# Projecting from a transposed input: five of eight blocks of a fused attention and mixture-of-LoRA layer

## The chip, the core and the metric

The kernel runs on one core of a Trainium2 chip. A core has a matrix engine (TensorE, "PE" in the profile; its weight loads are "PEld"), a vector engine (VectorE, "DVE"), a scalar engine (ScalarE, "ACT"), a general engine (GpSimd, "POOL") and a queue engine (SyncE, "SP") that here issues all DMAs. Each engine works through its own instructions in order; semaphores tie them together. The metric is the device time in microseconds of one execution, as the median of several runs. The profile is that of one execution.

## The reference

The input x has 2 sequences of 2048 rows of 512 numbers. All is in 32-bit floats. The layer is

```python
x = x + attention(layernorm(x), Wq, Wk, Wv, Wo)     # 16 heads of 32, causal, rotary positions
x = x + ffn(layernorm(x), base_w, base_b, router_w, router_b, lora_A, lora_B)
```

`layernorm` takes the mean from each row and divides by sqrt(variance + 1e-5). In the attention, q, k and v are the normalised rows times the transposed weights; q and k are then turned by position:

```python
rot = jnp.stack([t1 * cos - t2 * sin, t1 * sin + t2 * cos], axis=-1)
```

The feed-forward part is one dense product plus, for each row, the two best of eight LoRA experts, chosen by a softmax router.

## The kernel before

The 4096 rows are worked in eight blocks of 512 (four tiles of 128): blocks 0 to 3 are the first sequence, 4 to 7 the second. Block n has `j = n % 4`, and its queries look at the `j + 1` key blocks of their own sequence. The 16 heads are worked four at a time (index `g`, 0 to 3, one group of 32 rows of the matrix array for each head), so there are 32 head steps (n, g).

For each block, `prepare` (line 211) makes the normalised input with the channels on the partitions. `load` brings a tile of x; `measured` calls `moments` (line 175), which takes mean and variance on DVE, raises variance + eps to the power -0.5 on POOL and makes the shift -mean x factor on POOL; `scaled` normalises on ACT (line 189); `turned` makes four 128x128 transposes on TensorE (line 208) and copies the result from PSUM to `xnt_a` on ACT (line 209). `project` then makes keys and queries of one head group: 16 products of 128x32 weights in four column groups (line 201; after a turn in the same phase they run as four full products, line 196). The result is turned by position with a shuffle and a product with cosine on DVE (lines 251, 252) and a product with sine and a sum on POOL (lines 253, 254). `value` projects a tile of values and copies it from PSUM in four pieces on ACT (line 271).

For each head step, `row_maxima` makes all scores once to find the row maxima (line 424 on TensorE, line 442 on DVE), and `attend` makes them again the other way round (line 585), takes exponentials on ACT (line 627) into one of three `pt` buffers, multiplies them with the values (line 665) and adds them up on POOL (line 715); their sums go through DRAM (`sums`, `few`, `over`, lines 737 to 748) and come back to scale the result (line 750). `finish` (line 280) does the output projection, the second layer norm, the router and the feed-forward product of a block that has all its heads. Scores, projections and all other products take turns in seven PSUM banks, handed out in rotation; the weighted values have an eighth.

The order of the instructions on TensorE, ACT and DVE is the order in which the program writes them. A planner writes it: the work of the scores is cut into phases (`phase`, `begin[k]` the first phase of head step k), and everything else is put between them. `set_aside(at, do)` does something at a given phase; `wait([(us, do)], at, not_before)` gives work for TensorE with an estimated time, a due phase and an earliest phase, taken when there is credit for it or when it is due. The queues of POOL and SP are ordered by the compiler.

`start_block` (line 856) sets a block's preparation: with `at` the block's first phase and `lead` at most 12, but less where the last head step of the block before is short, tiles are loaded from phase `at - lead - 14`, measured two phases later, scaled two more later and turned from `at - lead - 9`; the projections can begin at `at - lead - 6`. `xnt_a`, `cos` and `sin` have one buffer each, so a block's load of them waits for the last use in the block before. The tag `tmp`, with six buffers, holds tiles of x, the shuffled projections, normalised rows of the feed-forward part and the sums. The tag `w`, one buffer of 1 MB, holds `wo` and `base_w` in turn.

Of the kernel before, what the change touches and what calls it, by code (L numbers as in the profile page):

```python
# [12 lines left out]
ALU = mybir.AluOpType  # L13
# [21 lines left out]
def preln_attention_moe_lora(  # L35
    ctx: ExitStack,
    tc: tile.TileContext,
    x: bass.AP,
    wq_t: bass.AP,
    wk_t: bass.AP,  # L40
# [128 lines left out]
    def load_in_turn(src, name):  # L169
# [3 lines left out]
        return w  # L173

    def moments(xt, t, name):

# [33 lines left out]

    def prepare(n):

        j = blocks[n][1]
        made = {"q": [], "k": [], "v": []}
        held = {"x": [], "by": []}

        def load(t):
            held["x"].append(first_x[t] if n == 0 else load_x(n, t, False))  # L220
            if t == NT - 1:
                held["turn"] = first_turn if n == 0 else load_turn(j)

        def measured(t):
            held["by"].append(moments(held["x"][t], t, f"a{n}"))

# [29 lines left out]
        def value(t):  # L256
# [13 lines left out]
            for g in range(NC):  # L270
                nc.scalar.copy(made["v"][g][:, t, :], pv[:, bass.ts(g, P)])

# [4 lines left out]
        ]  # L277
        return (load, measured, scaled, turned), heads, [[(3.6, lambda t=t: value(t))] for t in range(NT)], made

# [576 lines left out]
    def start_block(n):  # L856

        (load, measured, scaled, turned), heads, vals, made = prepare(n)
        keys[n], values[n], queries[n], contexts[n] = made["k"], made["v"], made["q"], []
        at, j = begin[NC * n], blocks[n][1]  # L860

        lead = min(LEAD, at - begin[NC * n - 1] - 6) if n > 0 else 0
        for t in range(NT):
            if n > 0:
                set_aside(at - lead - EARLY + t, lambda t=t: load(t))
                set_aside(at - lead - EARLY + 2 + t, lambda t=t: measured(t))
                set_aside(at - lead - EARLY + 4 + t, lambda t=t: scaled(t))
                wait([(0.5, lambda t=t: turned(t))], at - lead - 8 + t, at - lead - 9 + t)
            else:
                load(t)  # L870
        if n == 0:
            for do in (measured, scaled, turned):
                for t in range(NT):
                    do(t)
            make_masks_of_maxima()
        for g in range(NC):
# [10 lines left out]
            if g == 1:  # L887
                for stage in vals:
                    wait(stage, begin[NC * n + 1] + 1, at - lead - 6)

    def end_block(n):
# [7 lines left out]

    EARLY, BEHIND, LEAD = 14, 3, 12  # L900
    start_block(0)
# [123 lines left out]
```

## Time and profile before

| | us |
|---|---|
| median of three runs | 1772.98 (1772.81 to 1774.18) |
| the profiled execution | 1771.69 |
| its span, first to last instruction | 1769.6 |
| TensorE busy | 1735.1 |
| DVE busy | 1016.9 |
| ACT busy | 763.5 |
| POOL busy | 1368.4 |
| granted TensorE clock | 0.997 of full |

The first row is the metric. The profile stands for one execution, whose own time is in the second row. Busy shares are means over the whole span: an engine with 77% can be the one that ends last in a stage, and an engine with 98% can have stages in which it waits.

In lines of groups, "x128 | 22.5, 305 | 8.4 <-ACT" reads: 128 instructions, 22.5 us busy together, 305 ns each, 8.4 us of idle time of the engine just before them, most of it ended by what follows the arrow. Matmuls overlap in the array, so their lengths add up to more than the time they take.

### The profile page before, as it was taken

The numbers are of one execution on the slowest core, as the hardware profiler recorded it, in microseconds if no ns is written. First come the engines' busy times: TensorE is split into PE (matmuls) and PEld (weight loads), VectorE is DVE, ScalarE is ACT, GpSimd is POOL, SyncE is SP. The second block draws the span as 40 slices with busy tenths as digits, with TensorE's granted clock in tenths as the row PEclk, the third lists the DMA queues.
The fourth block names the chain that finished last, engine by engine and source line by source line (L and its number), as shares of the span: only waits on it lengthen the run. The fifth ranks groups of instructions, "written<-read, shape, count | busy, mean of one in ns | idle before, by whom it ended". The sixth has DMA issues, their size and how long they took to land.

```text
span 1769.6 us, 45671 instructions
## 1 busy us (share of the span) xinstructions
PE 1735.1 (98%) x19482; PEld 694.9 (39%) x19482; DVE 1016.9 (57%) x2359; ACT 763.5 (43%) x1600; POOL 1368.4 (77%) x878
## 2 busy tenths in 40 slices
PE   8999999999999999999999999999999999999998
PEld 3444444333433334433343434333343433434333
DVE  4555655566657656564555556466565576666504
ACT  1434443345434535354542424334344445455371
POOL 3647766699797899899974478567996798999951
PEclk9999999999999999999999999999999999999999
DMA  5000101002110002200010121110022000010101
GB/s 191 20 15 21 61 26 56 8 8 67 45 36 8 8 2 67 71 10 2 20 33 14 44 73 62 43 44 4 14 71 67 1 9 8 2 32 20 61 8 48
DMA packets 42307, 61.91 MB, mean 35 GB/s; under 512 B 13180, under 2 KB 13692, under 8 KB 42104
## 3 DMA queue, kind: packets, MB, share of 16 engines
q1 hardware_dynamic: 42104, 59.00, 10.7%
q8 instruction: 152, 2.49, 0.6%
q14 instruction: 51, 0.42, 0.1%
HBM read 50.08 MB, written 8.90 MB: 33 GB/s over the span
## 4 chain that ended last, share of the span: by engine, by line
PE 45%; DVE 2%; POOL 1%; issue 1%; ACT 1%; DVEq 0%; POOLq 0%
PE sm L424 9%; PE av L665 8%; PE yps L196 4%; PE sc L585 4%; PE sc L609 4%; PE ops L201 3%; PE qps L201 3%; PE kps L201 2%; PE vps L201 2%; PE den L705 1%; PE yps L201 1%; PE sc L595 1%; POOL pt L715 1%; DVE pm L442 1%; PE mid L196 1%
## 5 line engine op out<-in xcount | busy, mean ns | idle before, releaser
L715 POOL TENSOR_TENSOR pt<-pt,pt 128x1024 f32<-128x1024 f32 (+3 forms) x544 | 1078.5, 2007 | 202.5 <-ACT pt L627 193.6
L627 ACT ACTIVATE pt<-sc 128x512 f32<-128x512 f32 (+1 forms) x1152 | 595.2, 573 | 804.7 <-PE sc L585 651.8
L442 DVE TENSOR_REDUCE pm<-sm 128x1 f32<-128x512 f32 (+3 forms) x1280 | 710.7, 604 | 346.8 <-PE sm L424 183.7
L424 PE MATMUL sm<-k,q 32*128 32x512 f32 (+3 forms) x2560 | 653.5, 571 | 2.4 <-ACT xnt_a L209 1.2
L585 PE MATMUL sc<-q,k 32*128 32x512 f32 (+3 forms) x2560 | 557.1, 540 | 0.0
L665 PE MATMUL av<-pt,v 128*32 128x256 f32 (+3 forms) x3392 | 317.1, 452 | 2.1 <-ACT ctx L684 1.4
L424 PEld LDWEIGHTS sm<-k,q 32*128 32x128 f32 x2560 | 246.4, 183 | 51.9 <-issue 28.8
L609 PE MATMUL sc<-max,ones_b 3*128 3x512 bf16 (+3 forms) x1648 | 211.8, 306 | 3.4 <-DVE pm L442 2.8
L585 PEld LDWEIGHTS sc<-q,k 32*128 32x128 f32 x2560 | 207.0, 185 | 5.6 <-issue 4.4
L665 PEld LDWEIGHTS av<-pt,v 128*32 128x32 f32 x3392 | 70.0, 108 | 242.7 <-issue 190.1
L609 PEld LDWEIGHTS <-ones_b 3*128 3x128 bf16 x1648 | 61.3, 91 | 184.7 <-issue 182.7
L201 PE MATMUL qps<-xnt_a,wq 128*32 128x512 f32 x992 | 114.0, 600 | 0.9 <-ACT pt L627 0.9
L201 PE MATMUL ops<-wo,ctx 128*32 128x512 f32 x896 | 101.1, 594 | 0.0
L201 PE MATMUL vps<-wv,xnt_a 128*32 128x512 f32 x864 | 97.9, 594 | 0.0
L201 PE MATMUL kps<-xnt_a,wk 128*32 128x512 f32 x800 | 90.9, 594 | 0.0
L196 PE MATMUL yps<-base_w,xnt_f 128*128 128x512 f32 x200 | 90.3, 594 | 0.6 <-DVE pm L442 0.6
L595 PEld LDWEIGHTS <-which 32*128 32x128 bf16 x2048 | 38.8, 91 | 120.2 <-issue 95.3
L253 POOL TENSOR_TENSOR sw_q<-sw_q,sin 128x512 f32<-128x512 f32 x32 | 41.0, 1281 | 53.6 <-DVE sw_q L251 53.6
L433 PEld LDWEIGHTS <-which_q 32*128 32x128 bf16 x2048 | 65.1, 92 | 25.1 <-issue 17.1
L253 POOL TENSOR_TENSOR sw_k<-sw_k,sin 128x512 f32<-128x512 f32 x32 | 40.9, 1279 | 40.5 <-DVE sw_k L251 40.5
L433 PE MATMUL sm<-past_q,which_q 32*128 32x32 bf16 x2048 | 70.3, 173 | 0.0
L386 DVE TENSOR_TENSOR xf<-yps,xf 128x512 f32<-128x512 f32 x32 | 22.1, 692 | 82.4 <-PE yps L196 52.4
(110 smaller groups left out, 1324.4 us busy)
## 6 DMA issues: line engine op xcount, KB each, us to landing
xa<-in_x SPq DMA_DIRECT2D x32, 256.0 KB
xf<-in_x SPq DMA_DIRECT2D x32, 256.0 KB
wo<-in_wo_t SPq DMA_DIRECT2D x8, 1024.0 KB
base_w<-in_base_wt SPq DMA_DIRECT2D x8, 1024.0 KB
out<-xf SPq DMA_DIRECT2D x32, 256.0 KB
sum<-over SPq DMA_DIRECT2D x124, 64.0 KB
cos<-in_cos SPq DMA_DIRECT2D x8, 256.0 KB
sin<-in_sin SPq DMA_DIRECT2D x8, 256.0 KB
```

The costliest lines, as they stand in the source:

```text
L196: nc.tensor.matmul(out=out, lhsT=lhsT, rhs=rhs, start=start, stop=stop)
L201: nc.tensor.matmul(out=out[rows, :], lhsT=lhsT[:, rows], rhs=rhs, start=start, stop=stop)
L253: nc.gpsimd.tensor_mul(sw, sw, held["turn"][1])
L424: nc.tensor.matmul(out=sc[r][:, some[i]], lhsT=q[rows, bass.ts(ts[i], P)], rhs=keys[c][rows, : wide_of[i]], start=(i == 0), stop=(c != j),)
L433: nc.tensor.matmul(out=sc[r][:, at : at + DK], lhsT=which_q[rows, DK * (3 - m) : DK * (3 - m) + P], rhs=past_q[rows, :], start=False, stop ...
L442: nc.vector.reduce_max(pm[:, t, r, c : c + 1], sc[r][:, here], axis=AX.X)
L585: nc.tensor.matmul(out=sc[r][:, place(kts[i])], lhsT=keys[jj][rows, bass.ts(tt, P)], rhs=q[rows, low(kts[i]) :], start=first(r), stop=(r n ...
L595: nc.tensor.matmul(out=sc[r][:, at : at + DK], lhsT=which[rows, DK * (3 - c) : DK * (3 - c) + P], rhs=past[rows, :], start=first(r), stop= ...
L609: nc.tensor.matmul(out=sc[r][:, at:end], lhsT=ones_b[rows, :], rhs=s["max"][rows, here : here + end - at], start=first(r), stop=(r in held ...
L627: nc.scalar.activation(pt[:, r, all_of], sc[r][:, all_of], AF.Exp, scale=1.0 / math.sqrt(DK))
L665: nc.tensor.matmul(out=s["av"][rows, lo:hi], lhsT=values[jj][g][:, tt, rows], rhs=pts[kt][:, r, at + lo : at + hi], start=(kt == 0 and lo ...
L715: nc.gpsimd.tensor_add(some, some, pts[kt][:, r : r + 2, place(kt)])
```

## The change

Five blocks (those with `lead` above 0: 2, 3, 4, 6 and 7) no longer turn normalised rows. A second copy of x, transposed by the host, is given as `x_t`; its 512 columns of the block are loaded straight to `xnt_a` (1 MB). They are neither centred nor scaled. Layer norm's mean is taken out of the weights instead: Wq, Wk and Wv are centred over their input channels on the chip once, in place, during block 1. For each weight, POOL adds the four chunks, TensorE multiplies the sum with ones, and DVE subtracts the mean. The factor 1/sqrt(variance + eps) of each row is still found from tiles of x (which are loaded two phases earlier and no longer scaled). It is written to DRAM as a row, read back on all 128 partitions and multiplied into the block's cosine and sine on POOL, which scales keys and queries; the values are scaled in their copy from PSUM. Blocks 0, 1 and 5 keep the old way.

```diff
+    def centre(w, name):
+        some = wide.tile([P, NC, D], F32, tag="w", name=f"some_{name}")
+        nc.gpsimd.tensor_add(some[:, :2, :], w[:, :2, :], w[:, 2:, :])
+        nc.gpsimd.tensor_add(some[:, 0, :], some[:, 0, :], some[:, 1, :])
+        def centred():
+            mean = bank(f"mean_{name}")
+            product(
+                out=mean, lhsT=one.to_broadcast([P, P]), rhs=some[:, 0, :], start=True, stop=True
+            )
+            nc.vector.scalar_tensor_tensor(
+                w, mean.unsqueeze(1).to_broadcast([P, NC, D]), -1.0 / D, w, ALU.mult, ALU.add
+            )
+        return centred
...
+        def load_turned():
+            held["xn_t"] = wide.tile([P, NC, BLK], F32, tag="xnt_a", name=f"xnt_a{n}")
+            nc.sync.dma_start(
+                out=held["xn_t"],
+                in_=x_t[:, bass.ds(b * S + j * BLK, BLK)].rearrange("(c p) s -> p c s", p=P),
+            )
...
+            rstd = held["rstd"][:, t : t + 1]
+            nc.vector.bn_stats(both[:, :n6], held["x"][t])
+            nc.vector.bn_aggr(both[:, n6:], both[:, :n6])
+            nc.vector.tensor_scalar_add(rstd, both[:, n6 + 1 : n6 + 2], EPS)
+            nc.gpsimd.tensor_tensor(rstd, rstd, power, ALU.pow)
+
+        def spread():
+            row = dram.tile([P, NT], F32, name=f"row_{n}")
+            nc.sync.dma_start(out=row, in_=held["rstd"])
+            held["row"] = p2.tile([P, BLK], F32, tag="tmp", bufs=6, name=f"rows_{n}")
+            nc.sync.dma_start(
+                out=held["row"],
+                in_=row.rearrange("(o p) t -> o (p t)", o=1).to_broadcast([P, BLK]),
+            )
+
+        def weighted_turn():
+            by = held["row"].rearrange("q (p t) -> q t p", t=NT)
+            for turn_of in held["turn"]:
+                some = turn_of.rearrange("q (t p) -> q t p", t=NT)
+                nc.gpsimd.tensor_mul(some, some, by)
...
             for g in range(NC):
-                nc.scalar.copy(made["v"][g][:, t, :], pv[:, bass.ts(g, P)])
+                if flat:
+                    nc.scalar.activation(
+                        made["v"][g][:, t, :], pv[:, bass.ts(g, P)], AF.Copy,
+                        scale=held["rstd"][:, t : t + 1],
+                    )
+                else:
+                    nc.scalar.copy(made["v"][g][:, t, :], pv[:, bass.ts(g, P)])
...
+        lead = min(LEAD, at - begin[NC * n - 1] - 6) if n > 0 else 0
+        flat = lead > 0
...
+            if flat:
+                set_aside(at - lead - EARLY - 2 + t, lambda t=t: load(t))
+                set_aside(at - lead - EARLY + t, lambda t=t: measured(t))
+            elif n > 0:
...
+        if flat:
+            set_aside(at - lead - EARLY + 3, spread)
+            set_aside(at - lead - EARLY + 5, load_turned)
+            set_aside(at - lead - 6, weighted_turn)
...
+        if n == 0:
+            for i, w in enumerate((wk, wq, wv)):
+                held = []
+                first = CENTRED + 4 * i
+                set_aside(first, lambda w=w, i=i, held=held: held.append(centre(w, i)))
+                wait([(0.9, lambda held=held: held.pop()())], first + 4, first + 2)
...
-    EARLY, BEHIND, LEAD = 14, 3, 12
+    EARLY, BEHIND, LEAD, CENTRED = 14, 3, 12, 22
...
+        "x_t": given("attn_x").reshape(B * S, D).T,
```

More of the change, by code (lines that the diff above doesn't have):

```diff
@@ L38, in preln_attention_moe_lora @@
     x: bass.AP,
+    x_t: bass.AP,
     wq_t: bass.AP,
@@ L209, in turn, with prepare @@
         nc.scalar.copy(xn_t[:, :, bass.ts(t, P)], tp.rearrange("p (c q) -> p c q", c=NC))
-    def prepare(n):
-        j = blocks[n][1]
+    def prepare(n, flat):
+        b, j = blocks[n]
         made = {"q": [], "k": [], "v": []}
@@ L222, in load @@
                 held["turn"] = first_turn if n == 0 else load_turn(j)
-        def measured(t):
-            held["by"].append(moments(held["x"][t], t, f"a{n}"))
+        def load_turned():
[4 more added lines that the diff above has]
+            )
+        def measured(t):
+            if not flat:
+                held["by"].append(moments(held["x"][t], t, f"a{n}"))
+                return
+            if t == 0:
+                held["rstd"] = small.tile([P, NT], F32, tag="rstd", bufs=1, name=f"rstd_{n}")
+            n6, n2 = nc.vector.BN_STATS_DIM, nc.vector.BN_AGGR_DIM
+            both = small.tile([P, n6 + n2], F32, tag="mom", bufs=4, name=f"mom_a{n}_{t}")
+            rstd = held["rstd"][:, t : t + 1]
[16 more added lines that the diff above has]
+                nc.gpsimd.tensor_mul(some, some, by)
         def scaled(t):
@@ L277, in prepare @@
         ]
-        return (load, measured, scaled, turned), heads, [[(3.6, lambda t=t: value(t))] for t in range(NT)], made
+        return (load, load_turned, measured, spread, weighted_turn, scaled, turned), heads, [[(3.6, lambda t=t: value(t))] for t in range(NT)], made
     def finish(n, ctx_t):
@@ L856, in start_block @@
     def start_block(n):
-        (load, measured, scaled, turned), heads, vals, made = prepare(n)
-        keys[n], values[n], queries[n], contexts[n] = made["k"], made["v"], made["q"], []
         at, j = begin[NC * n], blocks[n][1]
         lead = min(LEAD, at - begin[NC * n - 1] - 6) if n > 0 else 0
+        flat = lead > 0
+        pieces, heads, vals, made = prepare(n, flat)
+        load, load_turned, measured, spread, weighted_turn, scaled, turned = pieces
+        keys[n], values[n], queries[n], contexts[n] = made["k"], made["v"], made["q"], []
         for t in range(NT):
-            if n > 0:
+            if flat:
+                set_aside(at - lead - EARLY - 2 + t, lambda t=t: load(t))
+                set_aside(at - lead - EARLY + t, lambda t=t: measured(t))
+            elif n > 0:
                 set_aside(at - lead - EARLY + t, lambda t=t: load(t))
```

## The prediction

> **What bounds the kernel now.** I read the page first: span and busy shares, then the slices, then who waits for whom, then the groups of one shape each, then the time lines of the places that the change touches.
>
> ```profile
> span 1769.6 us, 45671 instructions
> PE 1735.1 (98%) x19482; PEld 694.9 (39%) x19482; DVE 1016.9 (57%) x2359; ACT 763.5 (43%) x1600; POOL 1368.4 (77%) x878
> POOL 3647766699797899899974478567996798999951
> ```
>
> TensorE (PE) is busy for 98% of the span, so work taken from it is time taken, unless something else ends last in that stage. POOL has an average of 77%, but slices of 9 in which it could be that something else. Next the groups:
>
> ```profile
> L208 PE MATMUL xnps_a<-ident,xa 128*128 128x128 f32 x128 | 22.5, 305 | 8.4 <-ACT xa L189 7.8 <-DVE three L454 0.2
> L209 ACT COPY xnt_a<-xnps_a 128x512 f32<-128x512 f32 x32 | 18.6, 592 | 7.3 <-PE xnps_a L208 7.2
> L189 ACT ACTIVATE xa<-xa,mom_a 128x512 f32<-128x512 f32 x32 | 26.4, 825 | 6.1 <-POOL mom_a L185 5.7 <-DVE mom_a L183 0.2
> L271 ACT COPY v<-vps 128x128 f32<-128x128 f32 x128 | 24.8, 279 | 102.1 <-PE vps L201 88.6 <-PE vps L196 13.4
> L715 POOL TENSOR_TENSOR pt<-pt,pt 128x1024 f32<-128x1024 f32 x360 | 846.1, 2381 | 146.9 <-ACT pt L627 143.0 <-DVE pt L516 1.2 <-PE av L665 1.2
> L253 POOL TENSOR_TENSOR sw_k<-sw_k,sin 128x512 f32<-128x512 f32 x32 | 40.9, 1279 | 40.5 <-DVE sw_k L251 40.5
> L252 DVE TENSOR_TENSOR k<-kps,cos 128x512 f32<-128x512 f32 x32 | 21.6, 675 | 0.0
> L185 POOL TENSOR_SCALAR mom_a<-mom_a 128x1 f32<-128x1 f32 x32 | 8.6, 268 | 3.2
> L344 ACT ACTIVATE ex<-logits,neg 128x8 f32<-128x8 f32 x32 | 10.3, 321 | 0.0
> ```
>
> The first line is what the change mostly removes. TensorE's time line shows what one of these turns costs where it stands:
>
> ```profile
> 468.81 0.40 PE L665 MATMUL av<-pt,v 128*32 128x256 f32 x4
> 469.14 0.66 PE L208 MATMUL xnps_a<-ident,xa 128*128 128x128 f32 x4
> 469.73 0.39 PE L609 MATMUL sc<-max,ones_b 3*128 3x512 bf16 x2
> ```
>
> The columns are start, length, engine, line. The av product ends at 469.21 and the next product begins at 469.73: four transposes put 0.52 us between them, less than their own 0.66, because both ends overlap.
>
> **Which blocks.** `lead` is min(12, phases in the last head step of the block before, less 6). It is 0 for blocks 1 and 5 (the blocks before them have one tile row) and above 0 for 2, 3, 4, 6, 7. These five lose 20 of the 32 turns. In the trace their turns begin at 219, 467, 763, 1091 and 1339 us.
>
> **The sum, term by term** (minus is time gained).
>
> 1. Transposes in blocks 2, 3, 6, 7: 16 x 0.52 = -8.3 us. All lie on TensorE.
>
> 2. Transposes in block 4: 4 x 0.52 = 2.1 us of TensorE, but here POOL ends last:
>
> ```profile
> 755.00:830.00 75.00, 73.76 (x796) 26.34 (x792) 42.56 (x82) 38.43 (x82) 73.89 (x44) 1.00 0.02 5
> ```
>
> This row of busy times by stage has PE, PEld, DVE, ACT, POOL: POOL is busy for 73.89 of 75 us, and just after that TensorE stands idle (2.46 us at 839.7 among others), while ScalarE (ACT) waits 4.87 us for POOL at 848. The change gives POOL two products of 128x512 (L253: 2 x 1.28 = 2.56) and takes four shifts (L185: 4 x 0.27, and some 0.1 idle after each, 1.5 in all). So POOL is 1.1 us later and TensorE 2.1 earlier. POOL was idle for 2.28 us at 830-832, which gives back part. I take -0.8; ends -2.1 and +1.1. One operand of those products steps 16 bytes, which no row here shows; L253 (both operands contiguous, 1.28 us) is the nearest row.
>
> [...]
>
> 3. Waits that go with the turns: TensorE idle 1.16 us at 227.9 (scores behind `xnt_a`, ACT's copy L209), 0.15, 0.08 and 0.15 us before turns (for L189), and 1.7 us at 1093 behind an ACT queue in which a removed L189/L209 pair (0.83 + 0.59) stood ahead of the feed-forward's copy, of which I take half: 1.16 + 0.37 + 0.85 = -2.4. Ends: 0 (next in line is VectorE's (DVE) row maximum, named at 230.3) and -3.2.
>
> 4. Three products for the weights' means: each is one chunk in four column groups, like a `den` product, which the chain shows as "0.86 PE den L705 x8" at 1692.38. 3 x 0.86 = +2.6, all on TensorE.
>
> 5. Three subtractions on DVE over 2048 columns, one operand in PSUM. L252 takes 675 ns for 512; the reductions (L442: 279 ns for 128, 684 for 512) give 1.055 ns a column; 675 + 1536 x 1.055 = 2.3 us each. Queued behind each are the row maxima that free the score banks, and TensorE waits for those. By the planner's due times they fall at phases 24 to 34, at about 119, 130 and 148 us. In 119-127 DVE is busy 7.41 of 8 us, so there most of 2.3 shows; I take 1.5. At 130 a 3.6 us projection on TensorE follows and DVE is then idle 3.73 us; 0.5. At 148 a projection has just ended; 0.5. Sum +2.5; ends 0 and 6.9.
>
> 6. POOL's sums of weight chunks, 2.38 (L715, 1024 columns) + 1.27 (512) = 3.65 us, three times, one to two phases ahead of the mean that needs them. POOL is busy 30.1 of 54 us at 105-159, with 9.0 us idle before 125.44: 0. Without that cover TensorE stands up to 3.65 each.
>
> 7. The row of factors. Four `pow` on POOL remain. Then 2 KB go out through SP's queue, come back as 256 KB, then POOL's two products, then the first key projection's product with cosine on DVE (L252), which had no POOL ahead of it. The sums' way through DRAM is the same kind of trip: `over` issued at 167.33, the next issue released at 168.80, 1.5 us; a 256 KB load moves at some 250 GB/s (209-215 us), 1 us: about 4 us with issues. The code leaves five phases, 2.6 us each at 763-771: 13 us. Next is POOL's own queue. In block 4 `sw_k` was ready at 777.8 and POOL came to it at 783.14, a backlog of 5.3 us, and DVE wants cosine at 777.73. The products stand about two POOL additions (4.7 us) ahead of that place, so cosine would be done at about 779.7, 2 us late; maxima behind it have slack, 0.8 to 0.9 us between them. I take +0.5; ends 0 and 5.3. At 250 and 470-475 us POOL is idle, so blocks 2, 3 (and 6, 7, alike) pay 0.
>
> 8. The values' copies become ACTIVATEs with a scale from memory. L344, 8 columns with one operand of that kind, takes 321 ns; the copies of 128 and 512 columns (279, 592) extrapolate to 181, so 0.14 us more each, 0.56 for the four of one tile, 20 times: 11 us more on ACT, against 20 x (0.83 + 0.59) = 28 less. Off the path, but exponentials queue behind them: +0.5; ends -2 and +3.
>
> 9. Loads. Five of 1 MB through SP; `base_w`, of the same size, was issued at 209.10 and the traffic falls off by 215-217. The x loads go two phases earlier and keep their buffers only until the statistics. The 1 MB load waits for the previous block's last read of `xnt_a`, three phases before first use, with `sums`, `over` and `out` behind it on SP. 0; end +3 in block 4, where the first projection follows soonest.
>
> -8.3 - 0.8 - 2.4 + 2.6 + 2.5 + 0 + 0.5 + 0.5 + 0 = -5.4 us. The profiled execution took 1771.69 (1769.6 span and 2.1 around it), so 1766.3 by its own time. It stood 1.3 below the median of the three runs shown; against that median the forecast is 1772.98 - 5.4 = **1767.6 us**.
>
> **The rivals.**
>
> *The gain is eaten.* Row maxima late behind all three subtractions (term 5 at 6.9 in place of 2.5) give 1772.0. For it: DVE 93% busy at 119-127. Against it: seven banks and the idle 3.73 us. Within 0.2%.
>
> *Slower: POOL stands at the two products.* They wait on a DMA in an in-order queue; SP, in order too, may hold the row behind a load that waits for its buffer. It did so before: SP issued at 198.52 and then nothing until 206.56, for the sine tile. All additions behind stop, and with three `pt` buffers ACT and TensorE follow. Place: the first phases of each flat block's lead. Price: the lateness past 13 us of slack, times five; from (5.4 + 3.5) / 5 = 1.8 us each it decides. 4 us each give 1787.6 less what POOL's idle time absorbs, say 1780. Against it: POOL waits for DMA at L750 only 18.2 us in 14 times, 2.5 at most.
>
> *Larger gain.* Terms 5, 7 and 8 at their favourable ends (0, 0, -2) and term 3 at -3.2: 1772.98 - 11.7 = 1761.3. For it: ACT is 17 us lighter just where feed-forward and projection share its queue.
>
> *It does not do what it says:* the planner gives less early filler, TensorE waits for maxima where a transpose stood. Terms 1 and 2 halve: 1772.1, counted with the eaten gain.
>
> **How the numbers follow.** Forecast 0.52, larger gain 0.12, eaten 0.16, slower 0.20. 0.2% of the time (3.5 us) is about what a measurement of this kernel tells from no change; below 1769.4 counts as faster. So faster 0.64, same 0.16, slower 0.20. The likeliest case alone spans 1763 to 1771. Leaving out some 0.06 below and 0.14 above, the range is 1759 to 1778.
>
> **What would show it.** [...] Wrong would be: DVE or POOL named in TensorE's waits at the flat blocks' first keys, POOL idle for a DMA at the new products, or SP standing still for longer than before.

## The result and the profile after

| | us |
|---|---|
| before, median of six runs beside it | 1772.89 (1771.46 to 1774.35) |
| after, median of six runs | 1783.67 (1781.66 to 1788.91) |
| ratio, 95% interval | 1.0069 (1.0059 to 1.0079) |
| the profiled execution after | 1787.35, span 1785.5, granted clock 0.996 |

The change makes the kernel 0.6 to 0.8% slower, some 11 us, where 5.4 us less was forecast. The page of after, span and busy times:

```profile
span 1785.5 us, 45395 instructions
PE 1730.9 (97%) x19360; PEld 687.4 (38%) x19360; DVE 1022.9 (57%) x2362; ACT 746.8 (42%) x1560; POOL 1388.5 (78%) x874
```

ACT is busy 17 us less, as the forecast had it. TensorE is busy 4 us less, where 7.8 follow from terms 1, 2 and 4 (10.4 - 2.6); the span is 16 us longer. So the loss is idle time and clock, not work. The groups of after that answer to the forecast's:

```profile
L226 PE MATMUL xnps_a<-ident,xa 128*128 128x128 f32 x48 | 9.3, 334 | 18.6 <-ACT xa L207 18.4 <-DVE three L511 0.2
L227 ACT COPY xnt_a<-xnps_a 128x512 f32<-128x512 f32 x12 | 6.7, 585 | 4.1 <-PE xnps_a L226 4.0
L207 ACT ACTIVATE xa<-xa,mom_a 128x512 f32<-128x512 f32 x12 | 9.8, 815 | 2.2 <-POOL mom_a L203 1.9 <-DVE mom_a L201 0.2
L323 ACT ACTIVATE v<-vps,rstd 128x128 f32<-128x128 f32 x80 | 22.9, 368 | 52.1 <-PE vps L219 41.4 <-PE vps L214 10.7
L187 DVE SCALAR_TENSOR_TENSOR wq<-mean,wq 128x2048 f32<-128x2048 f32 x1 | 2.3, 2281 | 0.0
L276 POOL TENSOR_TENSOR cos<-cos,rows 128x512 f32<-128x512 f32 x5 | 7.7, 1543 | 15.5 <-DMA rows<-row 13.2 <-DMA sum<-over 2.3
L179 POOL TENSOR_TENSOR some<-wk 128x1024 f32<-128x1024 f32 x1 | 2.3, 2339 | 7.9 <-DMA wk<-in_wk_t 7.9
```

The first five lines are as forecast: 48, 12 and 12 instructions are left, the subtraction takes 2.3 us, a value copy 368 ns (279 ns and 0.14 us more were forecast). The last two are not. POOL stands 15.5 us in front of its five cosine products, and 7.9 us in front of the first sum of weight chunks. TensorE's first line shows 18.6 us of waiting where there were 8.4 (for ACT 18.4, where there were 7.8).

**The start.** The time line of after, POOL first, then DVE, then TensorE:

```profile
1.43 0.30 POOL masks.py:199 TENSOR_SCALAR_AFFINE_SELECT ident<-ident 128x128 f32<-128x128 f32 x1
9.60 2.34 POOL L179 TENSOR_TENSOR some<-wk 128x1024 f32<-128x1024 f32 x1 [7.87 <-DMA wk<-in_wk_t]
11.89 1.03 POOL L90 TENSOR_SCALAR_AFFINE_SELECT past<-past 32x32 bf16<-32x32 bf16 x4
...
12.15 0.09 DVE L94 MEMSET past<- 1x32 bf16 x1 [10.02 <-POOL past L90]
...
18.45 4.07 PE L226 MATMUL xnps_a<-ident,xa 128*128 128x128 f32 x16 [18.45 <-ACT xa L207]
23.34 6.02 PE L214 MATMUL kps<-xnt_a,wk 128*128 128x512 f32 x8 [0.82 <-ACT xnt_a L227]
```

The same places before:

```profile
2.19 1.03 POOL L89 TENSOR_SCALAR_AFFINE_SELECT past<-past 32x32 bf16<-32x32 bf16 x4 [0.47 <-DVE past L86]
...
7.82 4.07 PE L208 MATMUL xnps_a<-ident,xa 128*128 128x128 f32 x16 [7.82 <-ACT xa L189]
12.71 3.70 PE L196 MATMUL kps<-xnt_a,wk 128*128 128x512 f32 x8 [0.82 <-ACT xnt_a L209]
```

The program writes the first weight sum at phase 22, about 115 us in. But POOL's queue is ordered by the compiler, and there the sum is at the head, in front of the mask builds. It waits for the weights' load until 9.60; the masks wait behind it, DVE waits for the masks with the row statistics behind, and TensorE begins at 18.45 instead of 7.82: 10.6 us. The first key projection takes 6.02 us instead of 3.70; the trace's first clock record, at full speed, begins at 28.04 us, before at 11.96. These 2.3 us are not the sum's doing. The kernel `centre_only` below has the same late start and this line:

```profile
23.64 3.70 PE L214 MATMUL kps<-xnt_a,wk 128*128 128x512 f32 x8 [0.81 <-ACT xnt_a L227]
```

And `flat_only`, which has no sums and starts at 7.8, takes 27.5 us for its 56 full key products, the first projection's among them, where the kernel before takes 25.7, and is 1.8 us late at its first score products. So with the same start of TensorE these products took 1.8 us more in one execution than in the other.

The sums that follow cost TensorE nothing here: its longest wait between 100 and 200 us is 0.42 us. The second sum waits, but not as the forecast feared:

```profile
135.02 2.35 POOL L179 TENSOR_TENSOR some<-wq 128x1024 f32<-128x1024 f32 x1 [5.68 <-PE mean L219]
```

Its scratch tile has one buffer (tag `w`), so it stands until TensorE's first mean product has read the sum before.

**Block 4.** POOL, SP, ACT and TensorE around the new products of after:

```profile
770.21 0.56 POOL L261 TENSOR_TENSOR rstd<-rstd,power 128x1 f32<-128x1 f32 x1
...
773.04 0.56 POOL L261 TENSOR_TENSOR rstd<-rstd,power 128x1 f32<-128x1 f32 x1
773.55 2.36 POOL L772 TENSOR_TENSOR pt<-pt,pt 128x1024 f32<-128x1024 f32 x1
779.06 1.57 POOL L276 TENSOR_TENSOR cos<-cos,rows 128x512 f32<-128x512 f32 x1 [3.14 <-DMA rows<-row]
...
773.62 0.33 SPq L265 DMA_DIRECT2D row<-rstd  x1
775.03 0.33 SPq L267 DMA_DIRECT2D rows<-row  x1
...
811.72 2.07 ACT L684 ACTIVATE pt<-sc 128x512 f32<-128x512 f32 x4 [5.11 <-POOL pt L772]
...
812.37 5.34 PE L219 MATMUL vps<-wv,xnt_a 128*32 128x512 f32 x32 [3.26 <-ACT pt L684]
```

The powers stand between POOL's additions, so the last is done at 773.6 and the row leaves SP at 773.62. The cosine product is only one addition behind the last power in POOL's queue: POOL is ready for it at 775.92 and stands for 3.14 us. POOL comes to this block's first `sw_k` at 797.25, before at 783.14. TensorE's score products are 7 to 8 us later here, so POOL has lost another 6 to 7: 3.14 of it is the stand and 3.1 the two products' own length. ACT waits for POOL for 6.49 us at 786.79 and for 5.11 at 811.72, which it did nowhere there before, and TensorE behind it for 1.33 and 3.26 us. Between 780 and 892 TensorE's waits come to 11.8 us, where the kernel before has 4.7. The others of over a us aren't shown to be POOL's: one of 2.45 stands in the kernel before as well (2.46 at 839.7), and two of 1.57 and 1.59 us, for DVE, come and go among the kernels below whether block 4 is flat or not. A table by stretch of after (start and end, length, busy time of PE, PEld, DVE, ACT and POOL, then the granted clock in the third column from the right) shows what follows such an idle time:

```profile
807.00:812.00 5.00, 2.10 (x18) 0.44 (x12) 2.42 (x4) 0.28 (x1) 5.00 (x4) 1.00 0.00 0
813.20:816.40 3.20, 3.20 (x20) 0.85 (x16) 0.00 (x0) 0.58 (x2) 3.20 (x3) 0.50 0.02 5
```

TensorE idle in the first stretch, POOL busy throughout; then half clock, for 3.41 us by the clock's records. Here a loss of 3.3 us costs some 1.7 more: the 32 value products at 812.37 take 5.34 us, and 32 others at 824.77 take 3.64.

**Block 6.** ACT's line in front of the second large wait, 2.41 us of TensorE at 1113:

```profile
1112.47 0.81 ACT L207 ACTIVATE xn_f<-xf,mom_f 128x512 f32<-128x512 f32 x1 [4.39 <-POOL mom_f L203]
```

POOL stands 2.36 us for the row until 1108.55 and then works the two products; the power and the shift that ACT's normalising of the feed-forward rows needs are queued behind them.

### The profile page after: what moved, and what is told of

It is laid out like the page before. It is cut to its first block, busy times and chain, and to the rows that moved or that the text cites. A ratio compares the mean times of both kernels' runs of the same rounds, so it can differ in the third digit from the quotient of the medians.

```text
span 1785.5 us, 45395 instructions
## 1 busy us (share of the span) xinstructions
PE 1730.9 (97%) x19360; PEld 687.4 (38%) x19360; DVE 1022.9 (57%) x2362; ACT 746.8 (42%) x1560; POOL 1388.5 (78%) x874
## 4 chain that ended last, share of the span: by engine, by line
PE 87%; DVE 4%; issue 3%; POOL 3%; ACT 2%; DMA 1%; SPq 0%; POOLq 0%; DVEq 0%
PE sm L481 17%; PE av L722 14%; PE sc L642 7%; PE sc L666 7%; PE yps L214 7%; PE qps L219 6%; PE ops L219 5%; PE vps L219 5%; PE kps L219 5%; POOL pt L772 2%; PE sc L652 2%; PE den L762 2%; PE kps L214 1%; DVE pm L499 1%; PE sm L490 1%
## 5 line engine op out<-in xcount | busy, mean ns | idle before, releaser
L214 PE MATMUL yps<-base_w,xnt_f 128*128 128x512 f32 x216 | 97.6, 594 | 0.6 <-DVE pm L499 0.6
L219 PE MATMUL ops<-wo,ctx 128*32 128x512 f32 x864 | 97.5, 594 | 0.0
```

What stands on the lines that cost most here:

```text
L214: nc.tensor.matmul(out=out, lhsT=lhsT, rhs=rhs, start=start, stop=stop)
L219: nc.tensor.matmul(out=out[rows, :], lhsT=lhsT[:, rows], rhs=rhs, start=start, stop=stop)
```

## The experiments

All ratios are to the kernel before, run beside them on the same chip, with 95% intervals. An interval is some 2 us to either side; kernels from different groups ran on different chips, where the kernel before took 1772.0 to 1773.2 us, so differences of 2 us between kernels are not clear of noise. Where ledgers are spoken of, a profile's span is split into start (until TensorE's first instruction), TensorE's later idle time, the tail, half of the time at half clock, and the rest, called work.

### The parts alone

Centring without the flat blocks (`flat = False` in `start_block`):

> The centring of the weights alone: no block takes the transposed x, all eight turn normalised rows as before (centred weights give the same projections of centred rows). Theory: the start costs 12.9 us, three mean products 2.7 and the subtractions on VectorE 0 to 2.5 that TensorE waits for: 1772.9 + 15.6 to 18.1, about 1789 us. Rival (the start is absorbed): 1776 to 1779.

Measured 1784.23 us, 1.0061 (1.0048 to 1.0074). Work is 1733.0 us against 1729.9, +3.1 (the three mean products were forecast at +2.6), and the start is 18.8 against 7.8. So neither expectation's range holds (about 1789; 1776 to 1779): the late start is not absorbed, and less is paid behind it. Centring alone makes the whole loss, and nearly all of it is the start.

The flat blocks without centring:

```diff
-        if n == 0:
+        if n < 0:
             for i, w in enumerate((wk, wq, wv)):
```

> The five blocks on the transposed x with the row factors, without the centring of the weights (so the mean of each row is left out of the computation in those five blocks: the weights stay as loaded). Theory: no late start, no mean products; 16 transposes groups at 0.52 and their waits gained (some 10.5 us), and 6 to 8 us lost where POOL stands for the row of factors in block 4: 1768 to 1770 us. Rival (the rows' way costs more than the transposes in every block): above 1773. If the forecast was right but for the start: 1763.

Measured 1773.0 us, 1.0000 (0.9990 to 1.0009). Work falls to 1719.9 us, by 10.0: the 20 turns of 0.52 us (10.4) are saved just as forecast. And nothing of it is left: idle time is 29.4 us against 22.9, time at half clock 21.0 against 10.2. At the first score product for the maxima of head step (3, 0) the profile is 10.2 us ahead of before's; at that of (4, 0), after block 4's preparation, 1.8. The time is 3 us above the theory's range and at the edge of the rival's (above 1773).

### The sums' place in POOL's queue

Sums tied behind the last addition that the program had written for POOL:

```diff
-        nc.gpsimd.tensor_add(some[:, :2, :], w[:, :2, :], w[:, 2:, :])
-        nc.gpsimd.tensor_add(some[:, 0, :], some[:, 0, :], some[:, 1, :])
+        with tc.issue_after(recent[0].ins):
+            nc.gpsimd.tensor_add(some[:, :2, :], w[:, :2, :], w[:, 2:, :])
+            nc.gpsimd.tensor_add(some[:, 0, :], some[:, 0, :], some[:, 1, :])
...
-            nc.gpsimd.tensor_add(dest, dest, sw)
+            recent[0] = nc.gpsimd.tensor_add(dest, dest, sw)
...
-                nc.gpsimd.tensor_add(some, some, pts[kt][:, r : r + 2, place(kt)])
+                recent[0] = nc.gpsimd.tensor_add(some, some, pts[kt][:, r : r + 2, place(kt)])
```

> The change as it is, but the chunk sums of the weights are queued on POOL behind the last addition that the program wrote before them, so that the first one cannot stand at the head of POOL's queue and wait for wk. Theory (POOL's queue order at the start): the first transpose begins at about 7.8 us instead of 18.4, the first key projection takes 3.7 us instead of 6.0, so 12.9 us less than the changed kernel: 1771 us. Rival (the loss lies in the subtractions on VectorE and in the rows' way through DRAM, and the late start is absorbed later, since POOL is behind anyway): no more than 4 us less, 1780 us. Third: the start is mended but block 4 loses what POOL stands at the products, so it ends level with the kernel before, 1771 to 1774, and not at the 1767.6 of the forecast.

Measured 1779.96 us, 1.0033 (1.0021 to 1.0045): the rival's number without its reason, for the start is 7.8 us again. But a new stand appears, here on POOL and on TensorE:

```profile
130.76 1.28 POOL L810 TENSOR_TENSOR ctx<-ctx,sum 128x512 f32<-128x512 f32 x1 [8.99 <-DMA sum<-over]
...
134.57 2.35 POOL L182 TENSOR_TENSOR some<-wq 128x1024 f32<-128x1024 f32 x1
136.99 1.26 POOL L183 TENSOR_TENSOR some<-some 128x512 f32<-128x512 f32 x1
...
138.31 1.20 PE L222 MATMUL mean<-some,one 128*32 128x512 f32 x8 [2.93 <-POOL some L183]
```

The idle time of 9 us on POOL that the forecast took as cover is a wait of POOL itself, here for a transfer, and in the kernel before for DVE:

```profile
125.44 1.27 POOL L253 TENSOR_TENSOR sw_q<-sw_q,sin 128x512 f32<-128x512 f32 x1 [9.04 <-DVE sw_q L251]
```

The sum of the query weights is queued behind the instruction that waits. The edit ties it there, behind the addition of `q` (133.34); the changed kernel has no such wait of TensorE. The gap of 8.99 us covered nothing that stood behind the instruction that ended it.

The first sum ten phases earlier (`first - 10 * (i == 0)`):

> As held_sums, but the first weight's chunk sums are written ten phases earlier (phase 12 instead of 22), so that they are done long before the mean product. Theory: in held_sums TensorE stood 2.9 us at 138 us for these sums, and the granted clock fell to half for 3.4 us behind that stand (1.7 us): both go, so 4.6 us less than held_sums' 1780, about 1775.5 us. Rival (the stand only moves to the next mean, or to the subtraction on VectorE): within 1.5 us of held_sums.

Measured 1779.31 us, 1.0047 (1.0033 to 1.0062). The stand is still there, 3.07 us at 138.8, and it is the second sum's: the rival.

### The row and the products in block 4

The products of cosine and sine on DVE, on top of the held sums (`nc.vector.tensor_mul(some, some, by)`):

> As held_sums, and the two products of cosine and sine with the row of factors are on VectorE instead of POOL, at the place in VectorE's order where the program writes them. Theory (POOL is what ends last in block 4, and its stand of 3.1 us for the row and its 3.1 us of products there are lost): 4 to 7 us less than held_sums, 1764 to 1767 us, and TensorE's idle time between 780 and 900 us falls from some 12 to some 5 us. Rival (VectorE now stands for the row in its place, and the row maxima with it): no gain over held_sums, or up to 4 us more.

Measured 1783.25 us, 1.0054 (1.0042 to 1.0066), 3.3 us slower than the held sums, as the rival had it. The wait of 3.26 us in block 4 is gone, but there are three new ones, of 2.10, 2.39 and 2.66 us, in which TensorE waits for DVE. DVE waited only 1.0 us for the row in all. The rest is in its products' lengths (DVE, POOL, TensorE of this kernel):

```profile
777.27 2.34 DVE L279 TENSOR_TENSOR cos<-cos,rows 128x512 f32<-128x512 f32 x1 [1.01 <-DMA rows<-row]
779.53 3.22 DVE L279 TENSOR_TENSOR sin<-sin,rows 128x512 f32<-128x512 f32 x1
...
773.93 13.36 POOL L775 TENSOR_TENSOR pt<-pt,pt 128x1024 f32<-128x1024 f32 x5
...
783.51 0.37 PE L669 MATMUL sc<-max,ones_b 3*128 3x512 bf16 x1 [2.39 <-DVE pm L502]
```

The five cosine products took 1.08 us at the least and in the median. Beside POOL's additions products took up to 3.22, although a cosine product at 241.44 took 1.08 us beside POOL's additions too. What makes some of them so long no run here shows.

Block 4 in the old way, with the early sum (`flat = lead > 0 and n != 4`):

> As early_sums, but block 4 keeps the old way (only blocks 2, 3, 6 and 7 take the transposed x). Theory (POOL ends last around block 4, and the new products and the stand for the row of factors there cost some 8 us against 2 us of transposes gained): TensorE's idle time between 770 and 890 us goes back from some 11 to some 5 us; 1768 to 1771 us, 5 to 7 less than early_sums. Rival (these waits come from the planner's other order of the projections, or from the values' copies): no more than 2 us less.

Measured 1780.11 us, 1.0036 (1.0024 to 1.0048), no different from five blocks (1779.31). The waits between 782 and 807 us are gone, but two of 1.57 and 1.59 come at 862.8 and 880, the pair that the changed kernel has with block 4 flat. Undecided, nearer the rival.

The row six phases earlier, with the early sum (tiles of x, statistics and `spread`; cosine, sine and `x_t` are then loaded together, one phase before their old place for `x_t`):

```diff
-                set_aside(at - lead - EARLY - 2 + t, lambda t=t: load(t))
-                set_aside(at - lead - EARLY + t, lambda t=t: measured(t))
+                set_aside(at - lead - EARLY - 8 + t, lambda t=t: load(t))
+                set_aside(at - lead - EARLY - 6 + t, lambda t=t: measured(t))
...
-            set_aside(at - lead - EARLY + 3, spread)
-            set_aside(at - lead - EARLY + 5, load_turned)
+            set_aside(at - lead - EARLY - 3, spread)
+            set_aside(at - lead - EARLY + 4, load_turned)
```

> As early_sums, but the flat blocks load and measure their tiles of x, and send the row of factors through DRAM, six phases earlier; cosine, sine and the transposed x are loaded where they were. Theory (POOL stands 13 us in four blocks at its product with cosine, since the row comes late behind other loads on SP): that stand goes to near 0, and TensorE's idle time around block 4 falls by about the 3.1 us that POOL stood there and the half clock behind it: 3 to 5 us less than early_sums, about 1771. Rival (it is the products' own 3.1 us on POOL that hurt, not the stand): no more than 2 us less.

Measured 1776.59 us, 1.0031 (1.0019 to 1.0043). That is 2.7 us less than with early sums alone, between the theory (3 to 5) and the rival (at most 2). In block 4 the waits fall to 1.61, 1.27 and 1.06, but POOL's stands for the row don't go: 16.6 us in three times.

Four empty entries of 0.5 us per flat block in the planner, so that its credit runs as before:

> As early_sums, and the planner of the flat blocks keeps the four entries of 0.5 us at the places of the former turns, but they do nothing: so TensorE's other work is put between the phases in the order of the kernel before. Theory (part of the new idle time comes from projections that the planner now takes earlier or later, as at 1510 us, where TensorE idles 3.2 us and 0.9 before): that idle time falls back to about 1, and the whole is 2 to 4 us less than early_sums. Rival (the idle time there comes from POOL alone): the 3.2 us stay, and the time is within 1.5 us of early_sums.

Measured 1779.87 us, 1.0045 (1.0033 to 1.0057), the time without them. The wait at 1510 us falls to 0.85 as the theory had it, but others come (1.42 at 480, 2.35 at 801.7, 3.09 at 1106.6). So the planner's credit moves waits about and isn't what the 7 us are lost to.

The two products alone, put into the kernel before, as multiplications by ones:

```diff
+        def weighted_turn():
+            for turn_of in held["turn"]:
+                nc.gpsimd.tensor_mul(turn_of, turn_of, one.to_broadcast([P, BLK]))
...
+        if n in (2, 3, 4, 6, 7):
+            set_aside(at - lead - 6, weighted_turn)
```

> The kernel before, with one thing added: in blocks 2, 3, 4, 6 and 7 GpSimd multiplies the block's cosine and sine by a column of ones, in place, at the place where the changed kernel multiplies them by the row factors. The output is that of the kernel before; there is no row, no centring and nothing saved. Theory (GpSimd's own work around a block's start is dear, since it ends last in block 4 and TensorE then waits for it): 10 products of 1.3 to 1.5 us, of which block 4's two and their like come back as TensorE's idle time, so slower by 3 to 7 us (1776 to 1780), with gaps of over 1 us between 760 and 900 us that the kernel before has not. Rival (the products lie beside other work, and only waiting for the row makes them late): within 1.5 us of the kernel before (1771.5 to 1774.5).

Measured 1781.8 us, 1.0053 (1.0041 to 1.0065): 9 us for ten products that take 1.04 us each. Neither theory had it. In block 4 not one of TensorE's waits changed. All the loss is in blocks 2 and 6 and in the clock. The lines of block 2 (POOL, ACT, TensorE, and the stretch behind with its clock):

```profile
209.87 1.04 POOL L229 TENSOR_TENSOR sin<-sin,one 128x512 f32<-128x512 f32 x1 [1.97 <-DMA sin<-in_sin]
...
229.59 0.81 ACT L189 ACTIVATE xa<-xa,mom_a 128x512 f32<-128x512 f32 x1 [5.22 <-POOL mom_a L185]
...
230.93 1.00 PE L428 MATMUL sm<-k,q 32*128 32x384 f32 x1 [4.11 <-ACT xnt_a L209]
...
229.50:239.60 10.10, 8.67 (x108) 5.99 (x110) 3.44 (x14) 5.31 (x12) 9.35 (x9) 0.50 0.01 2
```

POOL, in order, stood 1.97 us for the sine tile and spent 2.08 on the two products; 0.90 of this went into an idle time that it had before. 20 us further on it was 3.0 us late (the power in front of ACT's line begins at 228.63, before at 225.61), where ACT waits for POOL's powers and shifts. TensorE then stood 4.11 us (before: 1.16), and 10 us at half clock began within that wait. Here POOL's stand for a transfer and the products' length were paid together, where POOL was next wanted. In block 4 these products ran at 711, ahead of the stretch in which POOL is full, so the run doesn't acquit products that stand within it, as the changed kernel's do. (The changed kernel's ACT has no such powers of x to wait for in these blocks; those of the feed-forward rows remain, as block 6 shows.)

### Sums first

All three sums two phases apart at 72 to 98 us, ahead of POOL's long wait, in one shared scratch tile, with early rows:

```diff
-        some = wide.tile([P, NC, D], F32, tag="w", name=f"some_{name}")
+        if name == 0:
+            sums[0] = wide.tile([P, NC, D], F32, tag="w", name="some")
+        some = sums[0]
         with tc.issue_after(recent[0].ins):
-            nc.gpsimd.tensor_add(some[:, :2, :], w[:, :2, :], w[:, 2:, :])
-            nc.gpsimd.tensor_add(some[:, 0, :], some[:, 0, :], some[:, 1, :])
+            nc.gpsimd.tensor_add(some[:, name : name + 2, :], w[:, :2, :], w[:, 2:, :])
+            nc.gpsimd.tensor_add(some[:, name, :], some[:, name, :], some[:, name + 1, :])
...
-                set_aside(first - 10 * (i == 0), lambda w=w, i=i, held=held: held.append(centre(w, i)))
+                set_aside(CENTRED - 10 + 2 * i, lambda w=w, i=i, held=held: held.append(centre(w, i)))
```

> The kernel with the row taken six phases earlier, and with it all three weight sums done one after the other, two phases apart, before GpSimd's long idle time at 130 us (the three share one scratch tile); the mean products and the subtractions stay where they were. Theory (the sum of the query weights stood in GpSimd's queue behind an addition that waits for a transfer): the idle time of 3 us near 138 us goes, and with it one window of half clock (1.7), so 4 to 5 us less than the 1776.6 of the kernel with early rows: 1771 to 1773. Rival (GpSimd's other work of that stretch, additions of the sums of the weights' tiles, is made late by 11 us of sums in a row, and TensorE waits for that instead): 1775 to 1779.

Measured 1771.5 us, 0.9994 (0.9985 to 1.0004), as the theory said. Means and subtractions now cost some 2.8 us together (this profile's distance to before's, at the first score products for the maxima, goes from +0.3 at head step (0, 3) to +3.1 at (1, 2)); 5.1 was forecast for the two terms.

The same with the products on DVE:

> The same, with the two products of cosine and sine by the row on VectorE instead of GpSimd. With the row six phases earlier VectorE should no longer stand for it, as it did by 2.1 to 2.7 us a block when the products alone were moved. Theory (GpSimd's load in blocks 4 and 7 is what remains): 2 to 4 us less than the kernel with all sums first. Rival (VectorE's 10 products of some 0.7 us stand ahead of its maxima, or it still stands for the row): the same to 3 us more.

Measured 1780.11 us, 1.0040 (1.0028 to 1.0053), 8.6 us more than with the products on POOL and outside both expectations. The row is early now and DVE waits for it nowhere, yet its sine product in block 4 takes 3.33 us, beside additions on POOL. So it was not the row that made this product long.

The same with block 4 in the old way:

> The kernel with early rows and all sums first, with block 4 done as before the change (normalised and transposed on TensorE, so four blocks are flat and not five). Theory (block 4, where GpSimd ends last, gives its gain back): 1 to 3 us less than with five flat blocks. Rival (each block's place only moves the waits; the 2.1 us of four transposes saved in block 4 are lost): within 1.5 us of the kernel with five, or up to 2 us more.

Measured 1769.88 us, 0.9986 (0.9978 to 0.9995), 1.6 less than with five: the theory, at the small end of its range, though the two intervals overlap.

### The row's own share

Four kernels run side by side. Flat blocks without centring, row six phases earlier:

> The five flat blocks without the centring (which leaves the rows' means in, so the output isn't the reference's), with the row taken six phases earlier. Flat blocks alone took 1773.0, the time of the kernel before, although TensorE's work is 10 us shorter. Theory (the missing gain goes into engines that stand for the row of factors, whose chain is issued too late): 2 to 5 us less than the flat blocks alone, 1768 to 1771. Rival (TensorE's shorter work is caught up with by GpSimd's and ScalarE's own work in blocks 4 and 7, whenever the row comes): 1772 to 1774.

Measured 1768.95 us, 0.9980 (0.9970 to 0.9990), 4 less than the flat blocks alone: the theory. Sums first with the row in its old place:

> All three weight sums done early, with the row at the place that the changed kernel has. It splits the 12 us between the changed kernel and the kernel with sums first and early rows. Theory (both parts count): 1773 to 1775, so 9 to 11 us of the mending is the sums' place in GpSimd's queue and 2 to 3 the row's. Rival (the row's place mattered only while the sums made GpSimd late): within 1 us of 1771.5.

Measured 1775.28 us, 1.0013 (1.0003 to 1.0023): both parts count, the sums by 8.4 us (9 to 11 expected) and six phases of the row by 3.8 (2 to 3 expected). The changed kernel's profile is 12.9 us behind this one at the first score product and 12.3 at the last: what the sums' place costs it is the start. Blocks 4 and 7 in the old way (`n not in (4, 7)`):

> Sums first and early rows, with blocks 4 and 7 done as before the change, so three blocks flat (2, 3 and 6). Theory (block 7 too gives its gain back: gaps of 1.6, 1.0 and 0.6 us from 1500 us on, where the kernel before has one of 0.9): these gaps fall to the one, 2.3 us, against 2.1 of transposes lost: within 1 us of the 1769.9 with four blocks. Rival (the waits of block 7 only moved there and will come elsewhere): 1.5 to 3 us more than with four.

Measured 1768.16 us, 0.9977 (0.9967 to 0.9987), 1.7 less than with four, a little better than the theory: with the row six phases early, neither block is seen to gain by being flat, again with overlapping intervals. And all five blocks flat, with the row six phases earlier still (`EARLY - 14`, `- 12` and `- 9` in the three lines above):

> Sums first, five blocks flat, with the row another six phases earlier (twelve before the changed kernel's place). Theory (GpSimd's own work sets block 4's and 7's gaps, not the row): within 1 us of the 1771.5 of the kernel with sums first. Rival (the row is still late there): the gaps from 766 to 813 and from 1500 to 1510 us fall, 2 to 5 us less.

Measured 1767.67 us, 0.9973 (0.9962 to 0.9983). The rival holds here: the row was still late. POOL's waits with the row in its old place (us in all, times, longest):

```profile
POOL cos L283 <- DMA rows<-row: 14.6, 4, 4.5
```

and twelve phases earlier, with the page's span and busy times:

```profile
POOL cos L284 <- DMA rows<-row: 3.1, 1, 3.1
...
span 1762.7 us, 45401 instructions
PE 1725.4 (98%) x19360; PEld 684.9 (39%) x19360; DVE 1021.9 (58%) x2362; ACT 746.2 (42%) x1560; POOL 1387.3 (79%) x874
```

POOL does the same work as in the changed kernel, 1387 us, and the kernel is 16 us faster, 7.6 of them by the row: it was not POOL's load in all. Whether it was the standing or the products' place isn't told apart, because the compiler put the products earlier in POOL's queue as well. Block 4's now stand here, ahead of the stretch in which POOL is full (term 2):

```profile
732.11 1.52 POOL L284 TENSOR_TENSOR cos<-cos,rows 128x512 f32<-128x512 f32 x1 [3.12 <-DMA rows<-row]
733.59 1.57 POOL L284 TENSOR_TENSOR sin<-sin,rows 128x512 f32<-128x512 f32 x1
```

The statistics and powers come earlier too, and cosine and sine are loaded three phases later, so the 7.6 us are those of the whole chain. Where they are lost can be read by setting the same score products of the two profiles side by side. Up to block 4's preparation they stay within 0.5 us of each other. Around it the late row loses 8 us, in front of block 6 another 4; around blocks 2, 3 and 7 it loses nothing, although POOL stands for 2.9 to 4.5 us there too. With six phases only, POOL still stood for 16.3 us in three times, 9.45 of them in front of block 4's product. The waits between 760 and 815 us have gone with twelve. What remains are the pair for DVE, 1.59 us at 853.5 and 1.58 at 870.7, each with half clock behind it (the granted clock is 0.94 of full from 830 to 890 us), and in block 7 three waits that the row doesn't move:

```profile
1493.91 0.39 PE L674 MATMUL sc<-max,ones_b 3*128 3x512 bf16 x2 [1.57 <-ACT pt L692]
1498.53 0.39 PE L674 MATMUL sc<-max,ones_b 3*128 3x512 bf16 x2 [1.00 <-ACT pt L692]
1503.15 0.20 PE L660 MATMUL sc<-past,which 32*128 32x32 bf16 x3 [0.58 <-ACT pt L692]
```

Block 7 in the old way (`n != 7`), and blocks 4 and 7:

> The kernel with sums first and the row twelve phases earlier, with block 7 done as before the change (four flat blocks: 2, 3, 4, 6). Block 7's gaps of 1.57, 1.00 and 0.58 us stayed when the row came twelve phases earlier, so the row doesn't set them. Theory (they are block 7's transposes handed back as waits for other engines): one gap of 0.9 instead of 3.2 us, against 2.1 us of transposes lost: within 1 us of the 1767.7 with five. Rival (they would come in block 7 the old way too, or move): 1.5 to 3 us more.

> The same, with blocks 4 and 7 done as before the change (flat: 2, 3 and 6). Theory (the row's chain was the wait that block 4 lost by, so with the row early block 4 gains by being flat): 0.5 to 3 us more than with block 7 alone done the old way. Rival (block 4's gain goes to the two gaps of 1.58 us at 853 and 871 us and the windows of half clock behind them): 0 to 2 us less.

Measured 1761.27 us, 0.9947 (0.9933 to 0.9960), and 1766.79 us, 0.9965 (0.9951 to 0.9978). The first is the best kernel of the study, 0.4 to 0.7% faster than the kernel before. Its profile has two waits in block 7:

```profile
1498.67 0.39 PE L674 MATMUL sc<-max,ones_b 3*128 3x512 bf16 x2 [1.16 <-ACT pt L692]
1502.80 3.64 PE L226 MATMUL qps<-xnt_a,wq 128*32 128x512 f32 x32 [0.71 <-ACT pt L692]
```

That is 1.3 us less waiting against 2.1 us of turns put back; so the 6.4 us between the two medians are not explained by it. Neither run's expectations held: the first had "within 1 us" or slower, and the second is 5.5 us above the first, where 0.5 to 3 more or 0 to 2 less were expected. The execution profiled of the first was the slowest of its five, 1767.03, and the others took 1760.95 to 1764.65. With ranges of that width, that block 4 is worth being flat and block 7 not is likely, and by how much is open.

## Why the prediction was wrong

The forecast was 1767.6 us, faster; measured were 1783.67, slower and outside the range. Term by term:

- **Terms 1 and 2, the turns: right.** 10.4 us by 20 x 0.52; TensorE's work fell by 10.0 in the flat blocks alone. Term 2's reading that POOL ends last in block 4 was right too; but POOL was 6 to 7 us later there and not 1.1, with the stand of 3.14 us and the products' 3.1 both in it, and the runs don't separate the two.
- **Term 3, the waits that go with the turns: right once the row is early.** With the row twelve phases earlier both large ones, 1.16 us at 227.9 and 1.7 at 1093, are gone. With the row in its old place a wait of 2.54 us behind ACT stood at 1101 instead of the second.
- **Terms 4 and 5: right in size, exposure smaller.** The mean products take 1.06 us each with their overlaps (0.86), the subtractions 2.22 to 2.29 (2.3). Together they cost about 2.8 us where 5.1 was forecast, once the sums are in time.
- **Term 6, the sums of weight chunks, failed.** It read "0", with POOL's idle 9 us as cover. Two errors are in it. It took the phase at which the program writes an instruction for its place in POOL's queue, though POOL's queue is the compiler's: the first sum went to the head, in front of the mask builds, and cost the start 10.6 us. And the idle time was a wait of an instruction in front of the sum, which is no cover; the changed kernel didn't pay for this one, but the kernels with the sums tied did, 2.9 us of TensorE at 138. Doing the sums early while the row stays late gives 1783.67 - 1775.28 = 8.4 us by the medians.
- **Term 7, the row, failed in size: "+0.5".** The trip was put at 4 us and took 5.4 to 6.2 from the row's issue to the product's start (773.62 to 779.06 in block 4, 474.05 to 480.25 in block 3). The slack was put at five phases, 13 us. It was 2.3 us in block 4: the powers were late behind POOL's additions, and the products stood one addition behind them. POOL stood in all five blocks, 15.5 us. TensorE paid for it around blocks 4 and 6: that blocks 2, 3 and 7 would pay nothing was right, and that 6 would be like them was wrong. Twelve phases of earliness give 1775.28 - 1767.67 = 7.6 us by the medians.
- **Term 8:** the scaled copies take 368 ns instead of 279; ACT is 17 us lighter as worked out. Their exposure wasn't tried alone.
- **Term 9:** in block 2 SP stood from 214.6 to 220.16 for the `x_t` load's buffer, with a tile of x behind it. The row left at 232.47, right behind its last power on POOL, which ended at 232.44. The forecast named this queue for the rival and gave the term 0. How much of the row's lateness it made wasn't tried by itself.
- **Stride.** The forecast took 1.28 us for a POOL product, from L253 with both operands contiguous. With one operand stepping 16 bytes it took 1.53 (medians of 1529 and 1532 ns), about 20% more. For the ten products of five blocks that is 2.5 us of POOL's time.

The two failed terms together are 8.4 + 7.6 = 16.0 us, and the kernel with both mended takes 1767.67, which is the forecast's number. That it agrees to 0.1 is chance, since executions of one of these kernels spread over 5 us and more. By the profiles they are 12.3 and 10.8, for the changed kernel's profiled execution took 3.7 us more than its median and the last kernel's 3.2 less. The other terms are near but not exact: in this kernel's profile work is 9.8 us less than before, where 7.8 was forecast, and idle time 2.5 us more.

Of the rivals, the slower one described the row's part: POOL in order behind a DMA, decided from 1.8 us of lateness a block. It stood 2.3 to 3.9 us in each, in block 2 for `sum` at the last; three of the five stands were absorbed. The chance of 0.2 rested on the 13 us of slack and on POOL's mild waits for `sum`, both read from a trace in which these instructions had no place yet. The start had no rival at all.

The clock makes some of these losses larger, and was left out of the forecast: ahead of the tail the changed kernel's profile has four windows of 3.41 us at half clock in place of three, and the mean granted clock of the profiled execution, 0.997 before and 0.996 after, is 0.991 in `early_sums`.

## What to carry to other kernels

Ask of each added instruction which order its queue has and who wrote it. An instruction that the program writes late can be put first by whoever orders the queue, and then a wait for a load stands in front of everything else on that engine (7.87 us of POOL here, and a start 10.6 us later). Idle time in an in-order queue is cover only for what stands in front of the waiting instruction (in `held_sums` 8.99 us of it left TensorE a wait of 2.93); ask what ends it.

A result that goes through DRAM to an engine with a full queue needs its slack counted on that engine, in instructions between its last input and its use, not in phases of the plan (in block 4 the slack was 2.3 us there, and the trip took 5.4). When work leaves the bounding engine and the time doesn't fall, look for an engine that stands in order for a transfer, and move the transfer's source earlier before moving the work to another engine (six phases gained 3.8 us here, the products on DVE lost 8.6). If the waiting work moves with it, the gain is that of both.

## What the runs showed of the hardware

- Behind some of TensorE's waits the clock was at half. The kernel before has three such windows of 3.41 us ahead of its tail, from 230.41, 841.40 and 1093.98 us, behind waits of 1.16, 2.46 and 1.71 us. The changed kernel has four, from 813.10, 874.54, 891.61 and 1113.48, behind waits of 3.26, 1.57, 1.59 and 2.41. Its waits of 2.45 us until 852.2 and of 1.60 until 1518.2 have none behind them. In `products_alone` 10.1 us at half clock began within the wait of 4.11 us.
- DVE products of cosine and sine with the row, both operands in SBUF, took from 1.08 to 3.22 us in `dve_products` and from 1.07 to 3.33 in `sums_first_dve`. The longest of each ran beside POOL's additions, and so did one of 1.08 us and one of 1.27. The changed kernel's DVE product with one operand in PSUM (L303) has a mean of 675 ns.
- A POOL product with one operand stepping 16 bytes took 1.53 us (the changed kernel's L276), one with both contiguous 1.28 (before, L253), one with a column for the second operand 1.04 (`products_alone`, L229).
